# A readout's folds widened from 32 columns to all 128 columns of TensorE

## The chip, the cores and the metric

The kernel runs on one core of a Trainium2 chip. The metric is the device time of one execution in microseconds (us), the median of several runs. TensorE is called PE, VectorE DVE, ScalarE ACT, GpSimd POOL, and SyncE, which issues most DMAs here, SP.

## The reference

Eight images of 192 channels and 56 x 56 pixels go through four layers, each behind a group norm (32 groups) and added to what it was given: an involution (layer 0) and three selective state-space layers (1, 2, 3). All is float32, one sequence of 3136 pixels per image. Layer 1 runs its state-space part on three slices of 64 channels (512 inner channels each), layers 2 and 3 on 192 channels (384 inner channels). Every inner channel has 16 states. The heart of the three layers is the same:

```python
def step(h, inp):
    dt_t, B_t, C_t, x_t = inp
    h = h * jnp.exp(dt_t[..., None] * A) + (dt_t * x_t)[..., None] * B_t[:, None, :]
    return (h, jnp.einsum('nds,ns->nd', h, C_t))
h0 = jnp.zeros((N, D_INNER, D_STATE), x.dtype)
_, ys = jax.lax.scan(step, h0, (...))
y = ys.transpose(1, 0, 2) + xc * D
y = y * jax.nn.silu(z)
return y @ out_proj_W.T
```

The sum over the 16 states in the `einsum` is what the change concerns.

## The kernel before

A sequence is cut into 7 chunks of 448 pixels (T), so a layer has 56 chunks. The involution comes first, then each layer is one call of `ssm_layer`. Its jobs are chunks in layers 2 and 3 (56 jobs each) and slices of chunks in layer 1 (168 jobs). A job has nd = 4 (layer 1) or 3 groups (i, j) of 128 inner channels, and a group has four units (i, j, q), NQ = 4. A unit holds all 128 channels of the group and four of the 16 states: partition p of its tile `uhg[k]` is channel p // 4 of a block of 32 channels and state index p % 4, and its NR = 4 rows r are the four blocks. Layer 1 has 2688 units, layers 2 and 3 have 672 each, 4032 in all.

What a unit does, by name and line:

- `inputs_begin` (L773, ACT) puts the carried state ahead of the rows; `inputs_by_pool` (L786) or `inputs_by_vector` (L793, DVE) multiplies dt*x, spread over states in `reps`, by B. For DVE's units PE first spreads B into the bank `b` (`spread_b`, L753).
- `decays` (L765, ACT) writes exp(dt * A) into two banks `da`, four instructions a unit.
- `scan` (L797, DVE), twice a unit, runs two rows each; `keep` (L801, ACT) saves the last column.
- `readout` (L806, POOL) multiplies all four rows by C.
- `reduce` (PE) sums over the states. For the first unit of a group it takes the bank `y` and writes x * D into it (L812, `w.dd`), then for every unit it runs four folds (L815), one a row. A fold's weights add up the four partitions of a channel, and the 32 results of row r go to partitions 32r to 32r + 31 of the bank. Four units accumulate into one bank.
- `gated` (L831, DVE) multiplies a finished bank y into the gate `zs`. There is one bank for y and one for b, and two for the other matmuls (`mm_tile`).

The engines' queues are in order and written out by hand (`manual_schedule`). In the loop over units, unit k issues the reduce of unit k - 3, the first scan of k, the decays of k + 1, the inputs of k + 2 (POOL) or k + 1 (DVE), the readout of k - 2, the second scan of k, and so on. DVE's `gated` of a group comes ahead of the first scan of the fourth unit of the next group. The matmuls of the job that comes next (projections, convolution, gates) and of the job that has ended are `Step`s; `places` spreads them over the 2 x 16 or 2 x 12 half units of a job by a cost, and each step's `rest` (mostly an eviction by ACT) is issued one step behind its matmuls. `nothing` (L821) adds filler matmuls with zero weights to the bank y, one for each of up to three matmuls that a unit's plan lacks; they change no value.

Of the kernel before, what the change touches and what calls it, by code (L numbers as in the profile page):

```python
# [21 lines left out]
T = RC * WW  # L22
# [8 lines left out]
NR = NQ = 4  # L31
# [56 lines left out]
def conv_mamba_stack(ctx: ExitStack, tc: tile.TileContext, a, out):  # L88
    nc = tc.nc
# [8 lines left out]
    def const(shape, src=None, eng=None, dt=F32):  # L98
        n_const[0] += 1
        t = cst.tile(shape, dt, tag=f"k{n_const[0]}", name=f"k{n_const[0]}")  # L100
        if src is not None:
            (eng or nc.sync).dma_start(out=t, in_=src)
        return t
# [37 lines left out]

    fold = const([128, 32])
    nc.vector.tensor_reduce(fold, ident.rearrange("p (e n) -> p e n", n=4), mybir.AxisListType.X, ALU.add)

    def per_channel(name, p):
        return a[name].rearrange("(t p) -> p t", p=p)
# [566 lines left out]
    def ssm_layer(pool, w, jobs, n_slots):  # L713
# [21 lines left out]
        reps, brow, uhg, ys = {}, {}, {}, {}  # L735
# [72 lines left out]
        def reduce(k):  # L808
            i, j, q = units[k]
            if q == 0:  # L810
                ys[k // NQ] = banks.y.tile([128, 512], F32, tag="y", name="y")
                nc.tensor.matmul(ys[k // NQ][:, :T], lhsT=w.dd[:, j, :], rhs=us[i].xc[:, j, :], start=True, stop=False)  # L812
            y = ys[k // NQ]
            for r in range(NR):
                nc.tensor.matmul(y[32 * r : 32 * r + 32, :T], lhsT=fold, rhs=uhg[k][:, r, 1:], start=False, stop=(q == NQ - 1))  # L815

        def nothing(k, n):

# [68 lines left out]
        for k, (i, j, q) in enumerate(units):  # L887
# [29 lines left out]
            if k >= 3 and not melts:  # L917
                reduce(k - 3)
                nothing(k - 3, more > 2)
# [23 lines left out]
            if melts:  # L943
                reduce(k - 3)
                nothing(k - 3, (more > 2) + (more > 0))
# [15 lines left out]
        for k in range(n_units - 3, n_units):  # L961
            reduce(k)
# [342 lines left out]
```

## Time and profile before

| | |
|---|---|
| median of 3 runs | 24271.49 us (24245.45 to 24280.18) |
| profiled execution | 24248.1 us; span 24246.3 us, 1.8 us around it |
| mean granted TensorE clock | 0.851 |
| busy: DVE, POOL, PE, ACT | 95%, 94%, 86%, 70% |
| involution, until the first fold | 1615 us |
| layers 1, 2, 3, first fold to first fold of the next | 15079, 3874, 3678 us |

One execution was taken by the hardware profiler. A row of a group of instructions gives the line in the kernel, the engine, the operation, what is written and read, and a count; behind the bar the time in which the engine was busy with the group, the mean duration of one in ns, and the idle time just before them with what ended it. Matmuls are pipelined and their ends are modelled, so the spacing of their starts is a better measure than their durations. A float32 matmul is two PE instructions in the trace, a bfloat16 one is one. PEld are weight loads, which run beside matmuls. The clock is the share of the full TensorE clock that was granted.

### The profile page before, as it was taken

What the parts mean: (1) busy time and instruction counts of PE and PEld (TensorE: products, weight loads), DVE (VectorE), ACT (ScalarE), POOL (GpSimd) and SP (SyncE); (2) the same over time, 40 slices, a digit from 0 to 9 for tenths busy, and PEclk for the clock granted to TensorE, in tenths of its full rate; (3) what the DMA queues carried; (4) which work ended last, traced back from release to release, by engine and by line L of the source; (5) the groups of instructions that cost most, each with busy time, mean ns of one, the idle gap of its engine ahead of it and who ended that gap; (6) DMA issues with size and microseconds to landing.
All of it is one profiled execution on the core that took longest, in us unless ns stands there. A gap on an engine that the chain in (4) does not pass through costs nothing.

```text
span 24246.3 us, 240240 instructions
## 1 busy us (share of the span) xinstructions
PE 20737.2 (86%) x75311; PEld 6576.3 (27%) x75311; DVE 22923.2 (95%) x15658; ACT 17077.4 (70%) x32802; POOL 22744.0 (94%) x6775
## 2 busy tenths in 40 slices
PE   8988888888888888888888888888888988999988
PEld 2222222222222222222222222222333333333333
DVE  8989999999999999999999999997999998999999
ACT  2237777777777777777777777776777776777777
POOL 6679999999999999999999999997999998999999
PEclk9988877877877887788787887878999998999999
DMA  5433333333333333333333333333444443444444
GB/s 112 109 107 132 129 127 129 130 128 129 128 131 123 132 130 127 128 129 129 129 127 128 130 130 129 128 130 113 143 140 143 142 143 120 151 147 143 144 150 135
DMA packets 1209102, 3171.68 MB, mean 131 GB/s; under 512 B 166444, under 2 KB 470596, under 8 KB 1207688
## 3 DMA queue, kind: packets, MB, share of 16 engines
q1 hardware_dynamic: 1205016, 3155.25, 39.8%
q8 instruction: 591, 9.68, 0.2%
q14 instruction: 695, 5.69, 0.1%
q10 hardware_dynamic: 2800, 1.06, 0.0%
HBM read 2438.45 MB, written 555.55 MB: 123 GB/s over the span
## 4 chain that ended last, share of the span: by engine, by line
DVE 37%; PE 23%; ACT 13%; issue 13%; POOL 8%; DMA 5%; SPq 1%; DVEq 0%; POOLq 0%; ACTq 0%
DVE uhg L797 24%; DVE uhg L793 8%; ACT da L765 5%; POOL uhg L806 5%; PE y L815 3%; DMA rep<-ops 3%; POOL uhg L786 3%; PE mm L656 2%; PE mm L1117 2%; PE mm L622 2%; ACT L590 2%; PE mm L430 1%; PE y L821 1%; DVE prod L442 1%; PE y_inv L468 1%
## 5 line engine op out<-in xcount | busy, mean ns | idle before, releaser
L797 DVE TENSOR_TENSOR_SCAN uhg<-da,uhg 128x898 f32<-128x898 f32 x8064 | 15902.8, 2009 | 572.9 <-ACT da L765 564.4
L806 POOL TENSOR_TENSOR uhg<-uhg,rows 128x1792 f32<-128x1792 f32 x4032 | 14732.1, 3674 | 391.1 <-ACT carry L801 380.4
L765 ACT ACTIVATE da<-rep,k 128x448 f32<-128x448 f32 x16128 | 10253.1, 636 | 1351.5 <-DVE uhg L797 977.3
L786 POOL TENSOR_TENSOR uhg<-rep,rows 128x1792 f32<-128x1792 f32 x1795 | 7161.6, 3990 | 504.6 <-DMA rep<-ops 359.2
L815 PE MATMUL y<-uhg,k 128*32 128x448 f32 x32256 | 4524.5, 635 | 245.1 <-POOL uhg L806 244.7
L793 DVE TENSOR_TENSOR uhg<-rep,b 128x1792 f32<-128x1792 f32 x2237 | 4463.8, 1995 | 189.0 <-PE b L753 112.0
L801 ACT COPY carry<-uhg 128x4 f32<-128x4 f32 x4032 | 783.1, 194 | 3341.6 <-DVE uhg L797 3249.7
L821 PE MATMUL y<-w_d,k 128*128 128x448 f32 (+1 forms) x5698 | 2621.2, 564 | 0.0
L812 PE MATMUL y<-xc,w_d 128*128 128x448 f32 x2016 | 1501.4, 840 | 875.6 <-DVE zs L831 875.6
L821 PEld LDWEIGHTS y<-w_d,k 128*128 128x128 f32 x5698 | 1090.5, 208 | 1727.7 <-issue 1680.7
L656 PE MATMUL mm<-dbl,w_dt 36*128 36x448 f32 (+1 forms) x2016 | 1303.5, 743 | 225.6 <-ACT k L638 225.5
L815 PEld LDWEIGHTS y<-uhg,k 128*32 128x32 f32 x32256 | 680.2, 114 | 2954.0 <-issue 1875.2
L1105 PE MATMUL mm<-xs,k 64*128 64x448 f32 x1344 | 861.6, 744 | 650.8 <-ACT zs L695 545.3
L1143 PE MATMUL mm<-v,w_in 96*128 96x448 f32 x2688 | 1270.0, 606 | 172.6 <-ACT zs L695 98.3
L1087 PE MATMUL mm<-xs,k 128*128 128x448 f32 x2688 | 1137.1, 563 | 43.9 <-ACT zs L695 27.6
L753 PE MATMUL b<-k,k 96*128 96x448 bf16 x2237 | 842.4, 377 | 319.5 <-DVE uhg L793 319.5
L668 PE MATMUL mm<-xc,k 128*128 128x448 f32 x2016 | 1005.3, 616 | 113.1 <-DVE dt L671 108.2
L1175 PE MATMUL mm<-xin,w_conv 128*128 128x448 f32 x2688 | 1088.2, 547 | 2.0 <-ACT xin L697 1.0
L442 DVE TENSOR_TENSOR prod<-mm,shifted 128x448 f32<-128x448 f32 x1680 | 928.2, 611 | 135.5 <-PE y_inv L468 60.9
L812 PEld LDWEIGHTS y<-xc,w_d 128*128 128x128 f32 x2016 | 438.2, 258 | 1692.1 <-DVE zs L831 1095.6
L450 POOL TENSOR_TENSOR x<-x,one 96x448 f32<-96x448 f32 x560 | 631.0, 1134 | 264.5 <-DVE one L442 246.9
L661 ACT ACTIVATE dt<-mm,k 128x448 f32<-128x448 f32 x1008 | 620.5, 626 | 348.6 <-PE mm L656 347.7
(140 smaller groups left out, 19835.9 us busy)
## 6 DMA issues: line engine op xcount, KB each, us to landing
rep<-ops SPq DMA_DIRECT2D x4032, 448.0 KB, 5.8
ops<-dt SPq DMA_DIRECT2D x1008, 448.0 KB, 3.2
rows<-bc SPq DMA_DIRECT2D x1960, 224.0 KB, 6.2
shifted<-xpad SPq DMA_DIRECT2D x672, 179.0 KB, 4.5
xg<-stream SPq DMA_DIRECT2D x168, 336.0 KB, 7.4
xr<-stream SPq DMA_DIRECT2D x168, 336.0 KB, 8.0
stream<-xr SPq DMA_DIRECT2D x112, 336.0 KB, 6.8
xs<-xg SPq DMA_DIRECT2D x224, 112.0 KB, 2.3
```

The source lines that it names most:

```text
L442: nc.vector.tensor_mul(prod.rearrange("p (h w) -> p h w", w=WW), fbs[item][: 128 if kind == "four" else CP, :T].rearrange("p (h w) -> p h ...
L656: nc.tensor.matmul(u.dps[j][:, :T], lhsT=w.dtw[:, j * 128 : (j + 1) * 128], rhs=u.dbl[:nk, :], start=True, stop=True)
L765: nc.scalar.activation(t[:, 64 + 449 * r : 512 + 449 * r], reps[k // NQ][:, 2 * h + r, 0, :], AF.Exp, scale=w.neg_a[:, j * NR + 2 * h + r, ...
L786: nc.gpsimd.tensor_mul(uhg[k][:, :, 1:], reps[k // NQ][:, :, 1, :], b)
L793: nc.vector.tensor_mul(uhg[k][:, :, 1:], reps[k // NQ][:, :, 1, :], b)
L797: nc.vector.tensor_tensor_scan(v, banks.da[h][:, 63:961], v, 0.0, ALU.mult, ALU.add)
L806: nc.gpsimd.tensor_mul(v, v, us[i].rows[1, q].unsqueeze(1).to_broadcast([128, NR, T]))
L812: nc.tensor.matmul(ys[k // NQ][:, :T], lhsT=w.dd[:, j, :], rhs=us[i].xc[:, j, :], start=True, stop=False)
L815: nc.tensor.matmul(y[32 * r : 32 * r + 32, :T], lhsT=fold, rhs=uhg[k][:, r, 1:], start=False, stop=(q == NQ - 1))
L821: nc.tensor.matmul(ys[k // NQ][:, : nd * 112], lhsT=zeros, rhs=w.dd.rearrange("p j e -> p (j e)")[:, : nd * 112], start=False, stop=False,)
L1087: nc.tensor.matmul(pm[:, :T], lhsT=w.inconv[:, k, j * 128 : (j + 1) * 128], rhs=ck.xs[:, i, 2 - 2 * k : 2 - 2 * k + T], start=(k == 0), st ...
L1143: nc.tensor.matmul(pm[:, :T], lhsT=w.inw[:, k, m * 128 : (m + 1) * 128], rhs=ck.v[:, k, :], start=(k == 0), stop=(k == NCT - 1),)
```

## The change

The fold's weights (128 x 32) are copied into a constant of four 128 x 128 matrices, zero but for the 32 columns of row r. Each of the four folds of a unit multiplies by the matrix of its row and adds into all 128 partitions of the bank; where the matrix has zeros, zeros are added. The last fold of the last unit alone closes the accumulation. Number, order and operands of everything else stay.

```diff
     fold = const([128, 32])
     nc.vector.tensor_reduce(fold, ident.rearrange("p (e n) -> p e n", n=4), mybir.AxisListType.X, ALU.add)
+    wide = const([128, 4, 128])
+    nc.vector.memset(wide, 0.0)
+    for r in range(4):
+        nc.vector.tensor_copy(wide[:, r, 32 * r : 32 * r + 32], fold)
...
             y = ys[k // NQ]
             for r in range(NR):
-                nc.tensor.matmul(y[32 * r : 32 * r + 32, :T], lhsT=fold, rhs=uhg[k][:, r, 1:], start=False, stop=(q == NQ - 1))
+                nc.tensor.matmul(
+                    y[:, :T], lhsT=wide[:, r, :], rhs=uhg[k][:, r, 1:], start=False, stop=(q == NQ - 1 and r == NR - 1)
+                )
```

## The prediction

> **What bounds the kernel now.** I read the page first: the engines' shares, the clock, the chain of work, and the costliest groups of instructions.
>
> ```profile
> PE 20737.2 (86%) x75311; PEld 6576.3 (27%) x75311; DVE 22923.2 (95%) x15658; ACT 17077.4 (70%) x32802; POOL 22744.0 (94%) x6775
> ...
> PEclk9988877877877887788787887878999998999999
> ...
> DVE 37%; PE 23%; ACT 13%; issue 13%; POOL 8%; DMA 5%; SPq 1%; DVEq 0%; POOLq 0%; ACTq 0%
> ...
> L797 DVE TENSOR_TENSOR_SCAN uhg<-da,uhg 128x898 f32<-128x898 f32 x8064 | 15902.8, 2009 | 572.9 <-ACT da L765 564.4
> L806 POOL TENSOR_TENSOR uhg<-uhg,rows 128x1792 f32<-128x1792 f32 x4032 | 14732.1, 3674 | 391.1 <-ACT carry L801 380.4
> ...
> L815 PE MATMUL y<-uhg,k 128*32 128x448 f32 x32256 | 4524.5, 635 | 245.1 <-POOL uhg L806 244.7
> ...
> L821 PE MATMUL y<-w_d,k 128*128 128x448 f32 (+1 forms) x5698 | 2621.2, 564 | 0.0
> ```
>
> DVE (the scans) and POOL (the products with C) bound it together, at 95% and 94%; PE is third at 86%, with a clock below full for most of the middle. The row of the fold, L815, is the one to look at twice. 32256 instructions (two for each of 16128 matmuls) of 635 ns each would be 20.5 ms one after the other, but the engine was busy with them for 4.5 ms: they run about 4.5 deep. L821, on all 128 columns, has 5698 x 564 ns = 3.2 ms in 2.6 ms. So four folds that go to four groups of 32 columns go through the array together.
>
> The second view is PE's timeline at the end of a job of layer 1, where the clock is full. It gives the spacing of instructions, which is what a queue pays (durations overlap).
>
> ```profile
> 15011.16 1.02 PE L821 MATMUL y<-w_d,k 128*128 128x448 f32 x2
> 15012.11 0.96 PE L815 MATMUL y<-uhg,k 128*32 128x448 f32 x8
> 15013.00 1.02 PE L668 MATMUL mm<-xc,k 128*128 128x448 f32 x2
> 15013.85 0.91 PE L821 MATMUL y<-w_d,k 128*128 128x448 f32 x2
> 15014.60 0.92 PE L668 MATMUL mm<-xc,k 128*128 128x448 f32 x2
> 15015.36 0.35 PE L753 MATMUL b<-k,k 96*128 96x448 bf16 x1
> 15015.64 0.96 PE L815 MATMUL y<-uhg,k 128*32 128x448 f32 x8
> 15016.53 0.96 PE L558 MATMUL mm<-y,k 64*64 64x448 f32 x2
> ```
>
> From the start of eight fold instructions to the next start there are 0.89 us (15012.11 to 15013.00, 15015.64 to 15016.53). Two instructions on all columns take 0.75 us (13.85 to 14.60), so 0.376 us each by the starts in the trace, with their weight loads hidden. The two right behind a fold take 0.85 us, 0.10 more. A bf16 one takes 0.19 us and L821's shorter form (336 columns) 0.283 us by the same reading of starts. At half clock the 0.376 us is 0.746 us.
>
> The third view is the table by stage: layers 1, 2 and 3 from the first fold of each, first all instructions, then L815 alone.
>
> ```profile
> 1615.00:16694.00 15079.00, 12569.64 (x40390) 3680.72 (x40393) 14378.02 (x8712) 10947.40 (x21013) 14650.50 (x3939) 0.80 0.38 128
> 16694.00:20568.00 3874.00, 3442.45 (x12196) 1260.67 (x12199) 3645.16 (x2260) 2930.12 (x5610) 3558.86 (x962) 0.92 0.42 139
> 20568.00:24246.00 3678.00, 3296.44 (x12060) 1206.69 (x12057) 3514.15 (x2058) 2860.06 (x5533) 3536.13 (x955) 0.95 0.44 144
> ...
> 1615.00:16694.00 15079.00, 3107.25 (x21508) 460.77 (x21512) 0.80 0.38 128
> 16694.00:20568.00 3874.00, 718.15 (x5380) 110.25 (x5384) 0.92 0.42 139
> 20568.00:24246.00 3678.00, 699.13 (x5376) 109.22 (x5373) 0.95 0.44 144
> ```
>
> First column after the length is PE busy with its count; the last three are clock, DMA share and GB/s. Layer 1 has 2688 units of 5.61 us, layers 2 and 3 have 672 each of 5.76 and 5.47 us. PE has 2.51 ms idle in layer 1 (0.93 us a unit), 0.43 and 0.38 ms in the others. The involution ahead of these stages has no fold of this kind.
>
> **What the change does, part by part.** The number and order of matmuls stay: four folds a unit, eight PE instructions, at the same places in PE's queue, with the same wait of the first on POOL's product. What goes is that they lie on four different column groups. A wide fold takes all 128 columns and all partitions of the bank, so the next must follow it as two L821s follow each other: 8 x 0.376 = 3.01 us a unit, against 0.89 + 0.10 = 0.99 us now. PE gets 2.02 us x 4032 = 8.1 ms of work more. The weight load grows from 32 columns (109 ns) to 128 columns as L821's, 0.19 us in the denser rows; those are hidden behind the 0.376 us and so should these be. The setup adds a memset and four small copies on DVE; the nearest larger row is the gate's 128x448 product, 0.59 us, so between 0 and 3 us once. I take 2.
>
> A gain is in there too: the 0.14 us that lie between a fold's eight instructions and the next matmul (0.89 against the 0.75 us of two rounds) and the 0.10 us after it vanish; they are netted above. [...]
>
> What hides the added work? Idle PE, and PE time that is long only because the clock was halved. I count PE's work after the change at full clock, by stage, from the counts above (bf16 ones are L753 and L634, 1791, 503 and 498 in the three stages; short L821s 1128 and 1142 in layers 2 and 3):
> layer 1: 38599 x 0.376 + 1791 x 0.19 us = 14.85 ms of 15.08;
> layer 2: 10565 x 0.376 + 1128 x 0.283 + 503 x 0.19 = 4.39 ms of 3.87;
> layer 3: 10420 x 0.376 + 1142 x 0.283 + 498 x 0.19 = 4.34 ms of 3.68.
> So layers 2 and 3 can't hold it: at least 0.51 + 0.66 = 1.17 ms are added, 25.42 ms in all. In layer 1 PE would be full to 98.5%, beside POOL at 97% and DVE at 95%.
>
> Layer 1 will not keep its pace with three full engines, because PE's queue is in order and little may run late. Behind a fold in that queue stand the job's matmuls of that half unit, the spread of B (L753) and the fillers (L821). ACT waits for the matmuls to evict them, and its decays (L765), which the next scan needs, stand behind these evictions; DVE waits for the spread of B and, at the start of each fourth unit, for the fold itself (gate, L831). With two banks for the job's matmuls and one each for y and B, PE can be late by what a unit leaves after its fold, some 5.6 - 3.0 = 2.6 us, less than a unit.
>
> So I went through the starts of the folds in the trace and, over blocks of 1, 2 or 4 units, took the larger of the time that the block has now and the matmuls it will have at full clock. Two blocks of two units from layer 2's timeline: from the fold at 18034.48 to that at 18046.62 there are 12.14 us; the work will be 16 x 0.376 (folds), 16 x 0.376 (L1175), 0.19 (B) and 0.75 (L812) = 12.98 us. From 18005.99 to 18013.30 there are 7.31 us; the work will be 6.02 + 6 x 0.376 + 6 x 0.283 = 9.97 us. Sums: 48 units of layer 1 (three jobs) have 267.2 us now and 281.1 by fours, 294.9 by twos, 311.2 by single units; 12 units of layer 2 have 67.6 now, then 78.5, 81.3, 82.6; of layer 3 65.6, then 77.9, 79.9, 80.6. There are 56 such stretches in each layer. By fours: 56 x (13.9 + 10.9 + 12.3) = +2.08 ms; by twos: 56 x (27.7 + 13.7 + 14.3) = +3.12 ms; by single units, no lateness allowed: 56 x (44.0 + 15.0 + 15.0) = +4.14 ms. A lateness of half a unit is nearer to two than to four, and the present times hold some half-clock stretches that would go, so I take three quarters of the way: +2.85 ms. On the profiled execution of 24248.1 us (span 24246.3, 1.8 us around it) this gives 27.10 ms. It stands 23 us below the median of the runs, 24271.5, which is nothing here.
>
> The clock is the open size. In the table it is 0.80 where PE is busy 83% of the time, 0.92 and 0.95 at 89 and 90%; with PE busy nearly all the time I extend that to between 0.97 and 1. [...]
>
> **The rivals.** First, the clock stays as it is: the same work at 0.80, 0.92 and 0.95 is 14.85 / 0.80 = 18.56, 4.77 and 4.56 ms, and with 1.62 ms ahead the whole is 29.5 ms. For it: layer 1 halves its clock 40% of the time in spite of the fillers (L821). Against it: the clock rises with PE's share from row to row. Chance 0.07.
>
> Second, faster. Waits for PE would get shorter if PE's clock rose and the wide folds cost no more than PE's idle time. ACT and DVE waits for PE matmuls sum to 0.55 ms in layer 1 and 0.56 ms in the others (list of waits); the half-clock share of them (0.40 and 0.13 of the time) is 0.22 + 0.07 = 0.3 ms, giving 23.95 ms. It decides if eight wide instructions take under 0.99 + 0.93 (idle of a unit) = 1.9 us in layer 1. The timeline's 0.376 us makes them 3.0. Chance 0.03.
>
> Third, nothing changes, because the folds weren't concurrent or the wide ones still are: 24.25 ms. The 0.89 us for eight, seen in both folds of the timeline, speaks against it, and L821, which like the wide fold writes every partition of the bank, goes one by one. Chance 0.02.
>
> **How the numbers follow.** PE becomes the bound, 25.4 to 28.4 ms (the floor and the sum by single units), chance 0.88, time 27.10 ms. For 8 in 10 I leave out the bare floor and go slightly above the single-unit sum for a clock that is not quite full: 25.75 to 28.5 ms. About 0.2% (50 us) is what a measurement of this kernel can tell from no change; slower than that 0.95, within it 0.02, faster 0.03.
>
> **What would show it.** After: L815 has the form 128*128 and is busy over 12 ms; eight of them take 3.0 us from start to start of the next; PE is above 95% busy, PEclk at 9 throughout; DVE and POOL fall to 83 to 87%, with the same durations of a scan and a product; waits that PE ends (ACT dt and xc evictions, DVE zs L831, b L753) head the list, and the chain is mostly PE. By stage, layers 2 and 3 lengthen by 18 to 24%, layer 1 by 5 to 12%. If layer 1 stays within 2%, the lateness allowed was larger than I took; if its clock stays near 0.8, the first rival holds; if eight wide folds take clearly under 3 us, the count of PE's work fails.

## The result and the profile after

The changed kernel takes 27694.26 us (median of 4 runs, 27684.32 to 27701.72) against 24273.65 us: a ratio of 1.1416, 95% interval 1.1402 to 1.143. The profiled execution took 27691.57 us with a span of 27689.7 us. The prediction was 27.10 ms, so 0.59 ms of the 3.42 ms were not foreseen.

The same lines of the page as before: shares, clock, the chain by engine and by line, and the groups of the scan, the product with C and the fold (their lines have moved to L801, L810 and L819).

```profile
PE 26538.4 (96%) x75311; PEld 11754.3 (42%) x75311; DVE 23060.1 (83%) x15663; ACT 17176.5 (62%) x32802; POOL 22785.0 (82%) x6775
...
PEclk9999999999999999999999999999999999999999
...
PE 86%; DVE 8%; issue 2%; ACT 2%; DMA 1%; POOL 0%; SPq 0%; DVEq 0%; ACTq 0%; POOLq 0%
PE y L819 42%; PE y L827 7%; DVE uhg L801 4%; PE mm L1093 4%; PE mm L1181 4%; PE y L816 4%; PE mm L1149 3%; PE mm L660 3%; PE mm L626 3%; PE mm L672 2%; PE mm L1123 2%; PE mm L1207 2%; PE mm L637 2%; PE mm L1111 2%; PE b L757 2%
...
L810 POOL TENSOR_TENSOR uhg<-uhg,rows 128x1792 f32<-128x1792 f32 x4032 | 14771.6, 3673 | 3852.9 <-ACT carry L805 3829.1
L801 DVE TENSOR_TENSOR_SCAN uhg<-da,uhg 128x898 f32<-128x898 f32 x8064 | 15900.6, 2009 | 545.7 <-ACT da L769 540.1
L819 PE MATMUL y<-uhg,k 128*128 128x448 f32 x32256 | 13188.0, 552 | 1.9 <-POOL uhg L810 1.8
```

DVE and POOL do the same work in the same time (2009 and 3673 ns) and are idle for the rest. The chain, spread over many engines before, is 86% PE, and the fold's line alone is 42% of it. A fold instruction has become shorter by its modelled duration (552 ns against 635 ns), and the line is busy for 13.2 ms in place of 4.5 ms: that is the whole change in two numbers, read together.

PE's timeline after, in full clock:

```profile
17519.65 0.92 PE L816 MATMUL y<-xc,w_d 128*128 128x448 f32 x2
17520.40 3.18 PE L819 MATMUL y<-uhg,k 128*128 128x448 f32 x8
17523.42 0.91 PE L827 MATMUL y<-w_d,k 128*128 128x448 f32 x2
17524.17 3.17 PE L819 MATMUL y<-uhg,k 128*128 128x448 f32 x8
17527.18 0.92 PE L672 MATMUL mm<-xc,k 128*128 128x448 f32 x2
...
17529.63 3.17 PE L819 MATMUL y<-uhg,k 128*128 128x448 f32 x8
17532.73 1.72 PE L562 MATMUL mm<-y,k 64*64 64x448 f32 x4
```

Eight fold instructions take 3.01 us from start to the next start (17524.17 to 17527.18), and what stands behind them takes 0.75 us without the 0.10 us of before. In front of a matmul of 64 columns a wide fold takes 3.10 us (17529.63 to 17532.73): there such an addition is new. By stage, all instructions and then the fold alone:

```profile
1616.00:18493.00 16877.00, 16026.37 (x40387) 7008.93 (x40386) 14426.80 (x8713) 11031.26 (x21012) 14678.92 (x3939) 0.97 0.34 114
18493.00:23186.00 4693.00, 4594.32 (x12192) 2172.95 (x12191) 3686.93 (x2260) 2938.88 (x5610) 3565.03 (x962) 0.98 0.35 115
23186.00:27690.00 4504.00, 4493.59 (x12061) 2142.98 (x12059) 3559.24 (x2058) 2866.10 (x5533) 3542.10 (x955) 0.99 0.36 118
...
1616.00:18493.00 16877.00, 8834.05 (x21506) 4179.50 (x21505) 0.97 0.34 114
18493.00:23186.00 4693.00, 2180.19 (x5377) 1029.85 (x5376) 0.98 0.35 115
23186.00:27690.00 4504.00, 2173.41 (x5376) 1024.82 (x5375) 0.99 0.36 118
```

Layer 1 is longer by 11.9%, layers 2 and 3 by 21 and 22%; the involution ends when it did. In layer 3 PE has 10 us idle in 4504: by the profile's busy time it is all but full there. The longest of the waits that PE ends:

```profile
DVE zs L837 <- PE y L819: 1640.6, 672, 11.4
...
ACT dt L665 <- PE mm L660: 962.7, 339, 4.6
DVE uhg L797 <- PE b L757: 905.0, 655, 2.6
```

The gate waits for the last fold of its group (93.3 us in all before), ACT for the job's matmuls, DVE for B behind them.

To see where 8 ms of added work went I took PE's starts in both traces apart. Each interval from one instruction to the next (for a fold, its eight together) is the instruction's own time at full clock (0.376, 0.283 or 0.19 us; 0.889 us for eight narrow fold instructions, 3.010 us for eight wide ones), then what half clock added to that, then a remainder, called a change of form up to 0.13 us and a wait above. For the three layers, in ms:

| | folds | other matmuls | changes of form | waits | half clock | sum |
|---|---|---|---|---|---|---|
| before | 3.58 | 11.41 | 0.96 | 4.01 | 2.67 | 22.63 |
| after | 12.14 | 11.41 | 0.72 | 1.29 | 0.52 | 26.07 |
| difference | +8.55 | 0 | -0.25 | -2.72 | -2.15 | +3.44 |

So 8.55 ms of folds came; 2.72 ms lay in time in which PE had waited and 2.15 ms were paid by the faster clock. The line between these two is drawn by the account: where an interval has both half clock and a wait, another way to divide it moves some 0.15 ms from the one to the other.

### The profile page after: what moved, and what is told of

It reads as the page before. It is cut to its first block, busy times and chain, and to the rows that moved or that the text cites. A ratio compares the mean times of both kernels' runs of the same rounds, so it can differ in the third digit from the quotient of the medians.

```text
span 27689.7 us, 240127 instructions
## 1 busy us (share of the span) xinstructions
PE 26538.4 (96%) x75311; PEld 11754.3 (42%) x75311; DVE 23060.1 (83%) x15663; ACT 17176.5 (62%) x32802; POOL 22785.0 (82%) x6775
## 4 chain that ended last, share of the span: by engine, by line
PE 86%; DVE 8%; issue 2%; ACT 2%; DMA 1%; POOL 0%; SPq 0%; DVEq 0%; ACTq 0%; POOLq 0%
PE y L819 42%; PE y L827 7%; DVE uhg L801 4%; PE mm L1093 4%; PE mm L1181 4%; PE y L816 4%; PE mm L1149 3%; PE mm L660 3%; PE mm L626 3%; PE mm L672 2%; PE mm L1123 2%; PE mm L1207 2%; PE mm L637 2%; PE mm L1111 2%; PE b L757 2%
## 5 line engine op out<-in xcount | busy, mean ns | idle before, releaser
L810 POOL TENSOR_TENSOR uhg<-uhg,rows 128x1792 f32<-128x1792 f32 x4032 | 14771.6, 3673 | 3852.9 <-ACT carry L805 3829.1
L801 DVE TENSOR_TENSOR_SCAN uhg<-da,uhg 128x898 f32<-128x898 f32 x8064 | 15900.6, 2009 | 545.7 <-ACT da L769 540.1
L819 PE MATMUL y<-uhg,k 128*128 128x448 f32 x32256 | 13188.0, 552 | 1.9 <-POOL uhg L810 1.8
L819 PEld LDWEIGHTS y<-uhg,k 128*128 128x128 f32 x32256 | 6234.5, 195 | 6115.9 <-issue 5955.5
L805 ACT COPY carry<-uhg 128x4 f32<-128x4 f32 x4032 | 782.2, 194 | 3754.5 <-DVE uhg L801 3727.0
L827 PE MATMUL y<-w_d,k 128*128 128x448 f32 (+1 forms) x5698 | 2302.9, 506 | 0.0
L837 DVE TENSOR_TENSOR zs<-zs,y 128x448 f32<-128x448 f32 x1008 | 616.3, 611 | 1640.9 <-PE y L819 1640.6
L816 PE MATMUL y<-xc,w_d 128*128 128x448 f32 x2016 | 1148.9, 655 | 418.2 <-DVE zs L837 418.2
L675 DVE TENSOR_TENSOR dt<-dt,mm 128x448 f32<-128x448 f32 x1008 | 619.9, 620 | 1052.4 <-PE mm L672 522.1
L1149 PE MATMUL mm<-v,w_in 96*128 96x448 f32 x2688 | 1119.2, 546 | 21.7 <-ACT v L335 9.2
L660 PE MATMUL mm<-dbl,w_dt 36*128 36x448 f32 (+1 forms) x2016 | 1006.5, 589 | 0.2 <-ACT k L642 0.2
L618 ACT ACTIVATE xc<-mm,k 128x448 f32<-128x448 f32 x1008 | 628.9, 629 | 529.1 <-PE mm L1093 313.7
L672 PE MATMUL mm<-xc,k 128*128 128x448 f32 x2016 | 872.7, 547 | 2.6 <-DVE dt L675 2.6
```

The costliest lines, as they stand in the source:

```text
L660: nc.tensor.matmul(u.dps[j][:, :T], lhsT=w.dtw[:, j * 128 : (j + 1) * 128], rhs=u.dbl[:nk, :], start=True, stop=True)
L801: nc.vector.tensor_tensor_scan(v, banks.da[h][:, 63:961], v, 0.0, ALU.mult, ALU.add)
L810: nc.gpsimd.tensor_mul(v, v, us[i].rows[1, q].unsqueeze(1).to_broadcast([128, NR, T]))
L819: nc.tensor.matmul(y[:, :T], lhsT=wide[:, r, :], rhs=uhg[k][:, r, 1:], start=False, stop=(q == NQ - 1 and r == NR - 1))
L827: nc.tensor.matmul(ys[k // NQ][:, : nd * 112], lhsT=zeros, rhs=w.dd.rearrange("p j e -> p (j e)")[:, : nd * 112], start=False, stop=False,)
L1149: nc.tensor.matmul(pm[:, :T], lhsT=w.inw[:, k, m * 128 : (m + 1) * 128], rhs=ck.v[:, k, :], start=(k == 0), stop=(k == NCT - 1),)
```

## The experiments

The times are of one execution each, but for the run with one zero matmul (four) and the kernel before without its fillers (five). The kernel before took 24247 to 24274 us beside them.

**Is it the columns?** The folds stay narrow, but share their columns in three units of four.

```diff
-                nc.tensor.matmul(y[32 * r : 32 * r + 32, :T], lhsT=fold, rhs=uhg[k][:, r, 1:], start=False, stop=(q == NQ - 1))
+                p = 32 * (q if q < NQ - 1 else r)
+                nc.tensor.matmul(y[p : p + 32, :T], lhsT=fold, rhs=uhg[k][:, r, 1:], start=False, stop=(q == NQ - 1))
```

> The folds stay 32 columns wide, but in three units of four all four of a unit go to the same 32 columns and partitions (block q); in the fourth unit they go to the four blocks as before. The sums of the rows are mixed up by it; the number, size and operands of the instructions are those of before. Theory A (folds overlap only if they lie on different column groups; the wide fold is dear because all four share the columns): in these units eight fold instructions take 8 x 0.376 = 3.0 us from start to start of the next, plus about 0.1 of switching, so PE gets three quarters of the change's work; about 25.4 to 26.2 ms. Theory B (narrow folds are cheap because they are narrow, wherever they go): 0.89 us as before and 24.25 ms.

Measured: 27552.61 us. PE's timeline, with three folds on one column group and one on four:

```profile
12011.62 3.20 PE L816 MATMUL y<-uhg,k 128*32 128x448 f32 x8
12014.75 3.27 PE L1088 MATMUL mm<-xs,k 128*128 128x448 f32 x8
12017.95 3.20 PE L816 MATMUL y<-uhg,k 128*32 128x448 f32 x8
12021.08 3.27 PE L1088 MATMUL mm<-xs,k 128*128 128x448 f32 x8
...
12024.48 0.96 PE L816 MATMUL y<-uhg,k 128*32 128x448 f32 x8
```

Layer 1 by stage, all instructions:

```profile
1602.00:18535.00 16933.00, 15815.97 (x40386) 4707.38 (x40385) 14429.59 (x8713) 11003.76 (x21013) 14677.14 (x3939) 0.91 0.33 114
```

From 12017.95 to 12021.08 there are 3.13 us for eight instructions on the same 32 columns. Theory B falls: narrow folds on shared columns cost what wide ones do, so it is the place that made them cheap. Theory A's time falls too, by over 1.3 ms. The account says why: against the changed kernel 1.78 ms of folds were saved, but changes of form took back 0.38 ms, waits 0.51 and half clock 0.77 ms (half clock for 0.17 of layer 1, where the changed kernel has 0.06). A sum of work forecasts PE's queue, not the time.

**Is it only the time in PE's queue?** Narrow folds, and as much work ahead of them as the wide ones add.

```diff
             y = ys[k // NQ]
+            for _ in range(3):
+                nc.tensor.matmul(y[:, :403], lhsT=zeros, rhs=uhg[k][:, 0, 1:404], start=False, stop=False)
             for r in range(NR):
```

> The narrow folds of before, and ahead of each unit's folds three more matmuls with zero weights over 403 columns of the same uhg row: 6 x 0.376 x 403/448 = 2.03 us of PE a unit, what the wide folds add, without touching the folds. Theory A (the change costs what it occupies PE for): about the change's time, 27.7 to 28.3 ms, the upper part because the folds' switching (0.24 us a unit) is still paid. Theory C (the wide folds cost something else too, such as adding into all partitions or a later release of uhg): clearly below, 25 to 27 ms.

Measured: 27952.12 us, and by stage, all instructions:

```profile
1636.00:18706.00 17070.00, 16154.61 (x56517) 6352.88 (x56515) 14435.99 (x8712) 11028.05 (x21013) 14692.46 (x3938) 0.96 0.33 113
18706.00:23393.00 4687.00, 4600.98 (x16231) 1966.98 (x16223) 3686.16 (x2260) 2939.51 (x5611) 3568.67 (x962) 0.99 0.35 115
23393.00:27950.00 4557.00, 4549.06 (x16086) 1956.05 (x16078) 3557.18 (x2056) 2864.39 (x5530) 3545.38 (x955) 0.99 0.35 116
```

The stages are those of the changed kernel within 1.2%, with a clock within 0.01 of theirs. The change costs what it occupies PE for. The zeros, too, go into all partitions of the bank and keep uhg for as long, so this run alone can't set theory C's two examples apart from the time in the queue. For the partitions the run with zeros into 32 of them does, below: 27901.35 us, the same within 0.2%. For uhg the changed kernel's list of waits does: the gate is the only one in it that waits for a fold. With these theory C falls.

**How much of a saving comes back?** The changed kernel without its fillers (the condition in `nothing` is made false).

> The changed kernel without its 2849 filler matmuls (5698 instructions: 3428 x 0.376 + 2270 x 0.283 = 1.93 ms of PE at full clock). Theory A: PE's queue is the bound in all three layers, so the time falls by all of it: 25.7 to 26.0 ms, the clock stays above 0.9. Theory D (the time comes from PE, ACT, DVE and POOL waiting for each other in turn, the heavy units above all; the fillers stand in light units): less than half of it, 26.8 to 27.6 ms. If the clock falls without fillers, 26.5 or more with a clock under 0.9.

Measured: 26599.79 us, between the two theories: 1.09 of 1.93 ms, 57%.

```profile
1613.00:17820.00 16207.00, 14887.86 (x36959) 6406.75 (x36958) 14404.18 (x8712) 11011.37 (x21013) 14674.24 (x3939) 0.96 0.35 119
17820.00:22323.00 4503.00, 4306.20 (x11063) 1973.09 (x11062) 3675.38 (x2260) 2933.02 (x5610) 3563.74 (x962) 0.97 0.36 120
22323.00:26598.00 4275.00, 4180.92 (x10919) 1921.59 (x10918) 3549.55 (x2058) 2860.70 (x5534) 3541.43 (x955) 0.99 0.37 124
```

The clock stays (0.96 to 0.99). By the account PE's waits grow by 0.8 ms, of which some 0.25 ms each are the first matmul of a bank y (L816), which waits for the gate, and a gate projection (L1111) that waits for ACT. Even where PE had been 95% busy and more, a microsecond of it was not a microsecond of the kernel.

**Half the columns.** Weights of 64 columns (`pair`), rows 0 and 1 into the lower half of the bank, 2 and 3 into the upper.

```diff
+            for r in (0, 2, 1, 3):
+                nc.tensor.matmul(
+                    y[64 * (r // 2) : 64 * (r // 2) + 64, :T], lhsT=pair[:, r % 2, :], rhs=uhg[k][:, r, 1:],
+                    start=False, stop=(q == NQ - 1 and r % 2 == 1),
+                )
```

> Weights padded with zeros to 64 columns, two rows of a unit share the lower 64 partitions and two the upper, in the order 0, 2, 1, 3, so that neighbours lie on different halves. Theory A: two at a time, eight instructions in 4 x 0.376 + 0.14 = 1.65 us; 0.75 us a unit more than before, which layer 1 (0.93 us idle a unit and a slow clock) holds and layers 2 and 3 nearly: 24.3 to 24.9 ms. Theory B' (only 32-column groups overlap, or padding itself costs): 3.0 us, 27 ms or more.

Measured: 25176.74 us. One fold and its follower:

```profile
12001.76 1.72 PE L819 MATMUL y<-uhg,k 128*64 128x448 f32 x8
12003.42 3.27 PE L1094 MATMUL mm<-xs,k 128*128 128x448 f32 x8
```

1.66 us, as theory A has it: two go at a time. The time is 0.28 ms above its range: the work I held to fit into idle PE time did not fit for free. Added folds are 3.09 ms by the account, waits gave 1.09 ms and the clock 1.09 ms; 0.91 ms stayed.

The same folds in the order 0, 1, 2, 3:

> The crossed pairs with their order changed to 0, 1, 2, 3: neighbours share a half of the columns. Theory F (matmuls start in the order of the queue, so fold 2, whose half is free, waits behind fold 1, whose half is not): fold 0 alone, 1 beside 2, 3 alone, 6 x 0.376 + 0.14 = 2.4 us, 25.6 to 26.5 ms. Theory R (a free half takes the next matmul that fits it): 1.65 us and 25.2 ms as crossed.

Measured: 25199.12 us, and the fold takes 1.66 us again (12003.87 to 12005.53):

```profile
12003.87 1.73 PE L819 MATMUL y<-uhg,k 128*64 128x448 f32 x8
12005.53 3.27 PE L1094 MATMUL mm<-xs,k 128*128 128x448 f32 x8
```

Theory R holds: between these two orders the order in which the folds are written doesn't matter.

**The same small dose in another way.**

```diff
             y = ys[k // NQ]
+            nc.tensor.matmul(y[:, :T], lhsT=zeros, rhs=uhg[k][:, 0, 1:], start=False, stop=False)
             for r in range(NR):
```

> The narrow folds of before, and ahead of each unit's folds one matmul with zero weights over all 448 columns: 0.75 us of PE a unit, about what the crossed pairs added (1.655 - 0.889 = 0.77 us), in another way. Theory A with the account of the runs so far: again about 25.0 to 25.4 ms. The prediction's second rival (added work that fits into PE's idle time raises the clock and shortens the waits for PE): 23.9 to 24.2 ms.

Measured: 25273.27 us, ratio 1.0423 (1.0408 to 1.0439). Layer 1:

```profile
1639.00:17251.00 15612.00, 13692.16 (x45766) 4511.52 (x45769) 14409.06 (x8713) 10983.42 (x21015) 14676.28 (x3939) 0.88 0.37 124
```

With 0.75 us a unit more, the clock of layer 1 rises from 0.80 to 0.88 and the kernel is slower by 4%. The prediction's second rival, that a fuller PE pays by its clock, falls with this: the clock does rise, and the time with it.

**What the clock is worth before.** The kernel before without its fillers.

> The kernel before without its fillers: 1.93 ms less of PE at full clock. PE isn't the bound there, so this tells what the clock is worth: if the fillers hold the clock up and that matters, the clock falls from 0.85 to about 0.75 and the time rises to 24.4 to 25.0 ms; if PE's place in the chain is one of occupancy, the time falls, 23.9 to 24.2 ms.

Measured: 24343.22 us, ratio 1.0037 (1.0023 to 1.0051).

```profile
1633.00:16696.00 15063.00, 11815.61 (x36957) 3218.14 (x36949) 14358.78 (x8712) 10953.13 (x21012) 14642.66 (x3939) 0.74 0.38 128
16696.00:20629.00 3933.00, 3278.00 (x11064) 1127.60 (x11063) 3645.44 (x2260) 2941.22 (x5611) 3557.87 (x962) 0.86 0.42 137
20629.00:24355.00 3726.00, 3155.54 (x10920) 1076.33 (x10918) 3513.68 (x2058) 2866.72 (x5534) 3535.99 (x955) 0.88 0.43 142
```

The clock falls from 0.80, 0.92 and 0.95 to 0.74, 0.86 and 0.88, PE is busy for 0.75, 0.16 and 0.14 ms less, and the time rises by 0.4%: neither of the two expected ranges holds, but the direction is that of the clock. In layer 1, where DVE and POOL are 95 and 97% busy, nothing is lost; layers 2 and 3 lose 1.5 and 1.3%.

**Does the granted clock follow the columns in use?** Three zero matmuls again, with 32 columns of weights (`zeros[:, :32]` into `y[:32, :403]`).

> The kernel with three zero matmuls a unit, but with zero weights of 32 columns into the lowest 32 partitions in place of 128 columns into all. It asks why the clock fell more often with narrow folds that share their columns (half clock for 0.17 of layer 1, PE busy 93%) than with wide folds or wide zeros (0.06 and 0.08). Theory G (the clock's gate sees how much of the array is used): half clock for over 0.12 of layer 1, and over 28.2 ms. Theory H (it sees busy time alone): 0.06 to 0.09 as with wide zeros, 27.6 to 28.0 ms (a little may overlap with the folds).

Measured: 27901.35 us; half clock for 0.10 of layer 1.

```profile
1626.00:18723.00 17097.00, 16206.28 (x56519) 5146.30 (x56520) 14430.08 (x8713) 11029.81 (x21013) 14684.82 (x3939) 0.95 0.33 113
```

The time is that of theory H; the clock lies just above its range and under that of G. That speaks against the columns as the main thing, without settling it; why folds on shared columns had 0.17 stays open. The timeline shows something else:

```profile
12004.73 1.88 PE L815 MATMUL y<-uhg,k 128*32 128x403 f32 x5
12006.11 0.58 PE L817 MATMUL y<-uhg,k 128*32 128x448 f32 x3
12006.44 0.50 PE L815 MATMUL y<-uhg,k 128*32 128x403 f32 x1
12006.51 1.19 PE L817 MATMUL y<-uhg,k 128*32 128x448 f32 x5
```

Six zero instructions (L815) stand ahead of eight fold instructions (L817) in the order written. Three of the folds began 0.33 us before the last zero. By the order of the kernel they are those whose columns the zeros leave free, while the zeros, all on the same 32 columns, follow each other at 0.34 us.

**Does it matter where the work lies?** The changed kernel with narrow folds in some places, chosen by the plan's matmuls (`load`) at the place where the fold is issued.

```diff
-                reduce(k - 3)
+                reduce(k - 3, load > 3.9)      # the other run: load < 1.5
```

> The changed kernel, with the narrow folds of before in the 1279 places of the loop where the plan has four or more matmuls of a job beside the folds, and wide folds elsewhere. That takes 1279 x (3.01 - 0.89 - 0.19 for going into and out of the narrow form) = 2.47 ms of work off PE. Theory A (only PE's sum counts): 57% of it comes back, as with the fillers of the wide kernel (1.09 of 1.93 ms), 26.2 to 26.4 ms. Theory L (PE can be late by less than a unit, so the heavy stretches set the time and light ones are partly idle): 80 to 100% comes back, 25.2 to 25.7 ms.

> The same, but narrow in the 1199 places where the plan has at most 1.3 matmuls of a job (fillers stand there too): 1199 x 1.93 = 2.31 ms off PE. Theory A: 57%, 26.3 to 26.5 ms, the same as with the heavy places. Theory L: 30 to 50% comes back, 26.5 to 27.0 ms.

Measured: 26351.19 us where the plan is heavy and 26437.32 us where it is light. The traces have 1271 and 1198 narrow units (10168 and 9584 instructions), so 2.45 and 2.31 ms of work were taken away. From the changed kernel's 27694 us 1.34 and 1.26 ms came back: 55 and 54%. Theory L falls, by 0.65 ms in the heavy places (in the light ones the time is 0.06 ms under its range); it was the picture behind the prediction's sum over blocks.

No run points to a version that beats the kernel before: every dose put into PE cost time, and the kernel before lost 0.4% without its fillers, at a lower clock (0.79 against 0.85).

## Why the prediction was right or wrong

**The mechanism.** Right. The row of the fold, 32256 instructions of 635 ns in 4.5 ms, was read as folds that run side by side, and the change as taking that away: 3.01 us a unit was forecast and is measured. Shared columns alone do it (3.13 us with narrow folds), and about equal work of another kind costs about the same (27.95 ms). Of the signs that were named, most hold (PE 96%, layer 1 longer by 11.9%, the others by 21 and 22%). POOL at 82% lies just under its 83 to 87%, and ahead of all waits that PE ends stands POOL's for ACT (L805, 3.83 ms).

**The covers.** The weight loads (0.189 us each in the median) are hidden: wide folds start 0.375 to 0.379 us apart at full clock. The setup moved the first fold by under 0.5 us. The 0.24 us of going into and out of the narrow form (0.14 + 0.10) came back for the most part: of the 0.97 ms that they are over 4032 units, 0.14 us a unit (0.56 ms) are counted here within the narrow fold's 0.889 us, and changes of form fell from 0.96 to 0.72 ms. The rest is missing, and the timeline shows one reason: a wide fold in front of a matmul of 64 columns takes 3.10 us, where the prediction had 3.01 throughout. Other changes stay: eight instructions of `128*36` (L626) take 3.13 us from start to the next start (17501.25 to 17504.38), as they did before, the eight wide folds 3.01.

The 0.24 us a unit of the narrow form spoke for the change. The 2.02 us a unit that the wide folds add, net of them, are eight times as much.

**The clock.** Forecast, as an estimate from the table of before, between 0.97 and 1, measured 0.97, 0.98 and 0.99. The first rival, the clock of before, is out. PE's work at the new clock grows less than its count: of 8.55 ms of folds, half clock paid 2.15 ms and waits 2.72 ms, which leaves the 3.44 ms.

**The size.** PE's work at full clock was put at 23.58 ms in the three layers; it is 23.54. On top of it the prediction left 1.9 ms for all that isn't work, and 2.53 ms are measured: 0.72 changes of form, 1.29 waits, 0.52 half clock. The step that was off is the sum over blocks, whose terms came out too small. It took 0.376 us for each matmul, so it had no place for the changes of form, though the 0.10 us behind each fold had been read from the timeline, and it took the clock as full. Together these are 1.24 ms, most of them in layer 1 (0.53 and 0.39 ms), where the forecast (three quarters of the way from fours to twos, taken stage by stage) of +1.36 ms became +1.80; layers 2 and 3, forecast at +0.73 and +0.77 ms, took +0.82 and +0.83.

**The picture behind the sum.** Wrong. It said that heavy stretches set the time and light ones have room. Taking folds away from heavy or from light places brings the same share (55 and 54%). What the runs show in its place is a coupling that is there in heavy and light places alike. That a sum built on this picture came within 0.59 ms is in part luck: it left too much for the waits (1.9 ms, 1.29 measured) and nothing for the changes of form and half clock (1.24 ms). Against the time of before, 0.75 to 0.77 us a unit (3.0 to 3.1 ms of PE) cost 0.9 to 1.0 ms; the changed kernel without fillers (8.55 - 1.93 = 6.6 ms) 2.3 to 2.4 ms; the change (8.55 ms) 3.4 ms; that is 29 to 34, 35 and 40% of the work, and 54 to 57% for what is taken away from the upper end. One run doesn't fit the last share: narrow folds on shared columns have 1.78 ms less of folds than the changed kernel and are only 0.14 ms faster. Which of the waits between PE, DVE and ACT carry it is not settled. The largest on PE's side is the bank y (L816 behind the gate, some 0.5 of 1.29 ms by the account, 0.42 ms by the list of waits of the changed kernel), and there is one such bank; a second one wasn't tried.

```profile
PE y L816 <- DVE zs L837: 418.2, 343, 2.3
```

**The other rivals.** Nothing changes: out by the timeline. Faster: out by the run with one zero matmul, which stays under the 1.9 us a unit named as the point of decision (0.99 + 0.75) and is slower by 4%. That point was wrong as well: idle time of PE was not room here.

## What to carry to other kernels

A group whose count times its mean is far above its busy time runs side by side (the narrow folds: 32256 x 635 ns = 20.5 ms, busy for 4.5 ms), and what an edit did to that outweighed everything else about it here; spacing of starts, not durations, tells what a queue pays (a fold's mean duration fell to 552 ns while its line's time rose to 13.2 ms). Zeros that pad weights to the full width were not free here: eight fold instructions took 3.01 us with them and 0.89 us without. An engine that is idle for 14% of the time, as PE was before, may still stand in the chain for a third of each microsecond it gets (29 to 34% here), so work put into its idle time has to be priced by a dose in a run, and forms that alternate can cost time at a change (here 0.09 us between a wide fold and a matmul of 64 columns, 0.10 us behind a narrow fold).

## What the runs showed of the hardware that was not expected

In these runs a matmul on free columns started ahead of one that was written before it and whose columns were busy: with the narrow zeros three folds began at 12006.11, 0.33 us before a zero matmul (12006.44) that was written ahead of them. Folds in the order 0, 1, 2, 3 on two halves took 1.66 us, as crossed ones did, where an estimate from starts in the written order was 2.4 us. So PE's queue, taken as in order before the result, was not so in these traces for starts on different columns (ends are modelled).

The clock didn't follow PE's busy share alone in these runs: in layer 1 it was 0.91 at 93% busy with narrow folds on shared columns, and 0.96 at 92% with wide folds and no fillers.
